# A convolution stack: the ninth tap's image in packed rows of 32 instead of a pitch of 34

## The chip, the core and the metric

The kernel runs on one core of a Trainium2 chip. The metric is the device time in microseconds of one execution; lower is better. In the profile PE is TensorE's matmul, PEld its weight load, DVE is VectorE, ACT is ScalarE, POOL is GpSimd and SP is SyncE.

## The reference

Four layers with residuals run on an image x of shape (4, 32, 32, 16). The first three are the same computation with their own weights:

```python
first = jnp.einsum('ijpq,bpqc->bijc', M2, inputs)
K = jnp.transpose(G, (2, 3, 4, 0, 1, 5)).reshape(kh, kw, c, h * w * f)
shifted = lax.conv_general_dilated(inputs, K, window_strides=(1, 1), padding='SAME', ...)
shifted = shifted.reshape(b, h, w, h, w, f)
diff = jax.nn.relu(inputs[:, :, :, None, None, :] - shifted)
second = jnp.einsum('ijpq,bpqijc->bijc', W2, diff)
return first - L * second
```

The inputs are group-normalised first. So there is, for each of the 1024 output places (i, j), a 3x3 convolution of the whole image with its own kernel G, a ReLU of its difference to the image, and a weighted sum over all 1024 places (p, q). The convolution has 9 taps x 16 channels, 144 rows of contraction, and 1024 x 16 output columns for each of the 4 images of the batch. The fourth layer filters with an impulse response obtained from Fourier transforms; it is a small part of the time.

## The kernel before

A layer runs over 128 blocks of 8 places and, within a block, over the 4 images of the batch: 512 steps a layer, 1536 in the three layers. One step (lines 533 to 558) fills a pair of PSUM banks, one bank for each half of the image (16 rows x 32 columns, 512 columns of output), and VectorE then does the minimum, the multiplication with the weights and the sum in one instruction, L550. Four such pairs of banks rotate.

The 144 rows of contraction don't fit 128 partitions, and the two halves of the image lie in the two halves of the partitions (rows 0 to 63 and 64 to 127, 4 taps x 16 channels each). So a step has three groups of matmuls, written at L542: `ga` with image tile 0 (taps 0, 1, 3, 4), `gb` with image tile 1 (taps 2, 5, 6, 7), both float32, and `gn` with image tile 2 for the ninth tap. The ninth tap alone would leave three quarters of its 64 rows unused; they hold its high and low pieces, so that gn can run in the reduced type float32r: slots of 16 rows with high, low, high, low pieces of the image meet high, high, low, low pieces of the weights (`prepare_g` cuts the weights, L464 and L468).

An image tile, `ims[a][k]`, belongs to a pair of images a = 0 or 1 and has the shape `[P, 4, 2, 4, 34]`: per partition 4 groups of rows l, 2 images b, 4 rows cc in a group, and a row of 34 floats. A matmul reads 32 of the 34: `rhs=im[rows, :, b % 2, :, :S]`, 4 x 4 rows of 32.

For layer 0 the host delivers the shifted images unnormalised in `raw`; `load_first` loads them on SP's queue, the ninth tap into a tile `nine`, and `first_images` normalises them. `last_tap` does the ninth on VectorE in three operations (L231, L233, L235), after which GpSimd clears the edges (L222). For layers 1 and 2 `make_image` does the work once for each pair a: `group_norm`, then `store_image`, then `load_image`. `store_image` normalises (L330), writes into `ys[a]` the image (`whole`, ACT), its high piece (DVE) and its low piece (DVE), each with a column of zeros on either side, copies the rows that neighbouring partitions need into `ye[a]` (POOL for one edge, ACT for the other), and stores both in DRAM as `img[a]`, `[10, C, 3, ROW]` with ROW = 2 x 4 x 34 = 272, on the queues of SP and ACT. `load_image` issues 24 loads in turn on the queues of SP, ACT and POOL; each brings one tap for one half from DRAM. The shift in x comes from the start of the read, `tap % 3`, the shift in y from the row of `img[a]`; 270 floats (RUN) for each l come as one run, the zeros between rows included.

The order of instructions is that of the code (a manual schedule). At a layer's end the last block is done for images 0 and 1 first and then for 2 and 3, and the first block of the next layer likewise, so the new image of pair 0 is made while TensorE works on pair 1 of the old layer, and the image of pair 1 while it works on pair 0 of the new one. `todo` and `step` thread these generators between the steps. `ys` and `ye` are zeroed once, in `impulse_response`.

Of the kernel before, what the change touches and what calls it, by code (L numbers as in the profile page):

```python
# [29 lines left out]
F32 = mybir.dt.float32  # L30
F32R = mybir.dt.float32r
AF = mybir.ActivationFunctionType
ALU = mybir.AluOpType
# [4 lines left out]
P = 128  # L38
B, C, S = 4, 16, 32
NBLK = 128  # L40
TAPS = [0, 1, 3, 4, 2, 5, 6, 7, 8]
ROW = 2 * 4 * 34
RUN = ROW - 2
GC = 8
NK = S // 2
NF = S * NK
# [9 lines left out]
def conv_stack_kernel(ctx, tc, x, raw, M, W, first_w, G, h0, coef, cst, dft, idp, idq, out):  # L56
    nc = tc.nc

    const = ctx.enter_context(tc.tile_pool(name="const", bufs=1))
# [3 lines left out]
    imp = ctx.enter_context(tc.tile_pool(name="image", bufs=1))  # L63
# [4 lines left out]
    dram = ctx.enter_context(tc.tile_pool(name="dram", bufs=1, space=DRAM))  # L68
# [19 lines left out]

    ys, ye, img = [], [], []
    for a in range(2):  # L90
        ys.append(const.tile([P, 3, 2, 4, 34], F32, name=f"y{a}"))
        ye.append(const.tile([P, 3, 2, 4, 34], F32, name=f"e{a}"))
        img.append(dram.tile([10, C, 3, ROW], F32, name=f"img{a}"))
    hd = dram.tile([8 + C * HLEN], F32, name="hd")
    fd = dram.tile([P, B, 2, 2, S], F32, name="fd")
    td = dram.tile([NK, 2, S, 2 * P], F32, name="td")
# [76 lines left out]
    ims, yc = {}, {}  # L173

    def image_tiles(a):


        ims[a] = [
            imp.tile([P, 4, 2, 4, 34], d, tag=f"im{a}{k}", name=f"im{a}{k}")
            for k, d in enumerate((F32, F32, F32R))  # L180
        ]

    def load_first(a, which, b=slice(0, 2)):

        if a not in ims:
            image_tiles(a)
            nine[a] = st.tile([P, 4, 2, 4, 34], F32, name=f"nine{a}")
        to = nine[a] if which == 2 else ims[a][which]
        nc.sync.dma_start(
            out=to[:, :, b].rearrange("p l b cc x -> p l (b cc x)"),  # L190
            in_=raw[:, a, which].rearrange("p (l b n) -> p l b n", l=4, b=2)[:, :, b].rearrange(
                "p l b n -> p l (b n)"
            ),
        )
# [131 lines left out]
    def normalise(a, xt, neg, rstd):  # L326
        yc[a] = work.tile([P, 2, NBLK], F32, tag=f"yc{a}", name=f"yc{a}")
        for b in range(2):
            at = slice(b, b + 1)
            nc.vector.tensor_scalar(yc[a][:, b], xt[:, b], neg[:, at], rstd[:, at], ALU.add, ALU.mult)  # L330

    def make_image(a, xt):

        xt = xt[:, 2 * a : 2 * a + 2]
        neg, rstd = yield from group_norm(xt)
        store_image(a, xt, neg, rstd)
        yield
        load_image(a)

    def store_image(a, xt, neg, rstd):  # L340
        split = lambda t: t.rearrange("p b (cc q) -> p b cc q", q=S)
        whole, hi, lo = (ys[a][:, k, :, :, 1:33] for k in range(3))
        normalise(a, xt, neg, rstd)
        y = yc[a]
        nc.vector.tensor_copy(hi.bitcast(F32R), split(y))
        nc.scalar.copy(whole, split(y))
        nc.vector.tensor_tensor(lo, split(y), hi, ALU.subtract)  # L347
        nc.gpsimd.tensor_copy(ye[a][96:, :, :, 1:, :], ys[a][96:, :, :, :3, :])  # L348
        nc.scalar.copy(ye[a][:32, :, :, :3, :], ys[a][:32, :, :, 1:, :])
        flat = lambda t: t.rearrange("p k b cc x -> p (k b cc x)")  # L350
        rows = img[a].rearrange("p c k x -> p c (k x)")
        nc.sync.dma_start(out=rows[1:9].rearrange("p c x -> (p c) x"), in_=flat(ys[a]))
        nc.scalar.dma_start(out=rows[0], in_=flat(ye[a][7 * C :]))
        nc.scalar.dma_start(out=rows[9], in_=flat(ye[a][:C]))

    def load_image(a):
        image_tiles(a)
        taps = [(n // 4, n % 4, 0, TAPS[n]) for n in range(8)]
        taps += [(2, n, 1 + n % 2, 8) for n in range(4)]
        jobs = [(half, *tap) for tap in taps for half in range(2)]  # L360

        jobs.sort(key=lambda job: job[4] // 3 == 2 * job[0])
        for n, (half, k, slot, which, tap) in enumerate(jobs):
            at, p = 64 * half + C * slot, 4 * half + tap // 3
            (nc.sync, nc.scalar, nc.gpsimd)[n % 3].dma_start(  # L365
                out=ims[a][k][at : at + C]
                .bitcast(F32)
                .rearrange("c l b cc x -> c l (b cc x)")[:, :, :RUN],
                in_=img[a][p : p + 4, :, which, tap % 3 : tap % 3 + RUN].rearrange(
                    "l c x -> c l x"  # L370
                ),
            )

    def load_m(mt, layer, pm):
# [3 lines left out]
    def first_term(layer, xt):  # L378

        ft = work.tile([P, 2, 8, S], F32, tag="ft", name="ft")  # L380
        with tc.tile_pool(name="mp", bufs=4) as mp:
# [10 lines left out]
            for pm in range(4, 8):  # L392
# [3 lines left out]
                yield  # L396
            for _ in range(GC - 4):
                yield
# [31 lines left out]
    def chunk(layer, ch):  # L430
        return layer + ch // (NBLK // GC), ch % (NBLK // GC)

    def load_g(layer, ch, parts=((slice(0, GC), "9ab", nc.sync, nc.sync, nc.sync),)):

        layer, ch = at = chunk(layer, ch)
        if layer == 3 or at in gr:
            return
        gr[at] = ga, gb, g9 = [
            pool.tile([P, GC, P], F32, tag=tag, name=tag) for pool, tag in ((gs, "ga"), (gs, "gb"), (gp, "g9"))
        ]  # L440
        flat = lambda t: t.rearrange("r n m -> r (n m)")
        operands = dict(zip("9ab", zip((g9, ga, gb), G[layer][ch])))
        for part, order, *queues in parts:
            for (t, src), queue in zip((operands[k] for k in order), queues):
                queue.dma_start(out=flat(t[:, part]), in_=src[:, part.start * P : part.stop * P])
                yield

    def prepare_g(layer, ch, part=slice(0, GC), engine=nc.gpsimd):


        at = chunk(layer, ch)
        if at[0] == 3 or (part.start == 0 and at in gt):
            return
        if part.start == 0:
            gt[at] = *gr[at][:2], gs.tile([P, GC, P], F32R, tag="gn", name="gn")
        ga, gb, gn = (t[:, part] for t in gt[at])
        g9 = gr[at][2][:, part]

        gv = ga.rearrange("r n (p f) -> r (n p) f", f=C)
        engine.tensor_tensor(  # L460
            gv, gv, mid.unsqueeze(1).to_broadcast([P, gv.shape[1], C]), ALU.subtract
        )
        yield
        nc.scalar.copy(gn, g9)  # L464
        yield
        for r in (32, 96):
            lo = gn[r : r + 32]
            nc.vector.tensor_tensor(lo, g9[r : r + 32], lo.bitcast(F32), ALU.subtract)  # L468
            yield
# [266 lines left out]
    nine = {}  # L736
    with tc.tile_pool(name="st", bufs=1) as st:
# [17 lines left out]
        for which in range(3):  # L755
            load_first(0, which, slice(0, 1))
        next(loads)
        for which in range(3):
            load_first(0, which, slice(1, 2))
# [4 lines left out]
        for which in range(3):  # L764
            load_first(1, which)
# [24 lines left out]
    def own(k, slot):  # L790

        y = lambda at: lambda cc: late["y3"][:, cc, at : at + 8]
        return [
            ("po" if tile == block else block, tile, y(31 - TQ * k - q + 8 * block), k, q)
            for tile, block, q in slot
        ]
# [13 lines left out]
    whole = [own(0, [(t, t, q) for t in range(4)]) for q in (2, 3)]  # L810
# [138 lines left out]
    for block in range(1, 4):  # L949
        for bank, tile in sorted(m for m in left if m[0] == block):  # L950
            row = xo[32 * block : 32 * block + 32].rearrange("n (r j) -> n r j", j=C)
            src = bank_of[block][32 * tile : 32 * tile + 32].rearrange("n (j r) -> n r j", j=C)
# [131 lines left out]
```

## Time and profile before

| | us |
|---|---|
| median of 3 runs | 3104.75 (3104.68 to 3104.94) |
| span of the profiled execution | 3103.0 |
| VectorE L550, mean of one (1536 of them) | 1.224 |
| its accumulator's read | 0.083 |
| ga, gb: TensorE records, mean | 0.590, 0.588 |
| gn: TensorE records, mean | 0.805 |
| weight loads of ga, gb, gn, mean | 0.187, 0.185, 0.186 |
| layers 1 and 2, `img` to `im` loads: 96 of 67.5 KB, from issue to landing | 5.4 median, 2.2 to 7.5 |
| store of `ys`: 4 of 408 KB, from issue to landing | 2.4 median |

The profile was taken in one execution, whose span lies 1.75 us below the median of the runs. A record of a matmul is longer than the time that it occupies the array, because successive matmuls overlap, and its end is modelled; the distance between starts tells what a pass takes. The two halves of a step run beside each other, some nanoseconds apart, so a pair of records is one pass. In a timeline each line has start, duration, engine, line, operation, operands and, in brackets, idle time before it with what ended it. TensorE's clock is granted in full throughout.

### The profile page before, as it was taken

To read this page: it belongs to the slowest core of one execution; us is meant where nothing else is said; L and a number is where in the kernel's file an instruction comes from. 1 tells how busy PE (TensorE), PEld (TensorE's weight loads), DVE (VectorE), ACT (ScalarE), POOL (GpSimd) and SP (SyncE) were. 2 spreads that over 40 slices of the span, in tenths; PEclk is the share of its full clock that TensorE was granted. 3 is DMA by queue.
4 is the path that set the end of the run, shared out by engine and by line. 5 is a ranking of instruction groups with operands and counts; after the bars stand their busy time and mean duration, and the time that the engine had idled before them with its cause. 6 is when DMAs were issued, how large, how long until landed. Compare 5 with 4: busy or idle time off the path is not lost.

```text
span 3103.0 us, 39162 instructions
## 1 busy us (share of the span) xinstructions
PE 3094.0 (100%) x16268; PEld 1618.2 (52%) x16268; DVE 2066.7 (67%) x3358; ACT 74.2 (2%) x93; POOL 239.6 (8%) x279
## 2 busy tenths in 40 slices
PE   9999999999999999999999999999999999999999
PEld 7854555555555554544545454555444545445454
DVE  7667666666667765666666666776666666666664
ACT  1000000000000000000000000000000000000000
POOL 1022220000000101000000000010100000000000
PEclk9999999999999999999999999999999999999999
DMA  7353443333332745333333333274644454445422
GB/s 231 102 146 89 108 115 95 89 89 95 102 89 62 158 129 129 89 89 95 102 89 89 95 102 89 62 152 128 144 100 97 100 113 104 97 95 119 95 44 42
DMA packets 71003, 322.46 MB, mean 104 GB/s; under 512 B 10409, under 2 KB 20393, under 8 KB 45481
## 3 DMA queue, kind: packets, MB, share of 16 engines
q1 hardware_dynamic: 60592, 302.24, 39.2%
q10 hardware_dynamic: 6152, 9.99, 1.8%
q0 software_dynamic: 4080, 7.72, 1.2%
q8 instruction: 127, 2.08, 0.3%
q14 instruction: 52, 0.42, 0.1%
HBM read 313.64 MB, written 6.28 MB: 103 GB/s over the span
## 4 chain that ended last, share of the span: by engine, by line
PE 100%; DMA 0%; DVE 0%; issue 0%; ACTq 0%; DVEq 0%; ACT 0%
PE pt L542 97%; PE pt L822 1%; PE pt L402 1%; PE pt L576 0%; DMA ga<-in_G_dram 0%; PE pt L649 0%; DVE junk L550 0%; PE pt L690 0%; PE pt L248 0%; DVE ga L460 0%; PE pt L121 0%; ACTq L81 0%; DVE xo L959 0%; DVE d L150 0%; DVE d L153 0%
## 5 line engine op out<-in xcount | busy, mean ns | idle before, releaser
L550 DVE SCALAR_TENSOR_TENSOR junk<-pt,w 128x1024 f32<-128x1024 f32 x1536 | 1880.6, 1224 | 989.0 <-PE pt L542 971.7
L542 PE MATMUL pt<-im,ga 64*128 64x512 f32 x6144 | 1607.4, 590 | 0.0
L542 PE MATMUL pt<-im,gb 64*128 64x512 f32 x6144 | 1600.6, 588 | 0.0
L542 PE MATMUL pt<-im,gn 64*128 64x512 f32 x3072 | 1276.0, 805 | 0.0
L542 PEld LDWEIGHTS pt<-im,gb 64*128 64x128 f32 x6144 | 636.7, 185 | 682.6 <-issue 672.4
L542 PEld LDWEIGHTS pt<-im,ga 64*128 64x128 f32 x6144 | 626.4, 187 | 409.2 <-DVE junk L550 278.3
L542 PEld LDWEIGHTS pt<-im,gn 64*128 64x128 f32 x3072 | 319.7, 186 | 340.3 <-issue 328.5
L460 POOL TENSOR_TENSOR ga<-ga,cs 128x1024 f32<-128x1024 f32 (+1 forms) x48 | 112.5, 2345 | 2025.8 <-DMA ga<-in_G_dram 2025.0
L550 DVE DVE_READ_ACCUMULATOR junk<-pt,w 128x1 f32 x1536 | 127.6, 83 | 0.0
L468 DVE TENSOR_TENSOR gn<-g,gn 32x1024 fp32r<-32x1024 f32 (+2 forms) x98 | 117.7, 1201 | 2.7 <-ACT gn L464 0.6
L464 ACT CAST gn<-g 128x1024 fp32r<-128x1024 f32 (+2 forms) x49 | 50.4, 1029 | 2256.5 <-PE pt L542 2088.2
L417 POOL DMA_DIRECT2D fd<-ft x48 | 25.3, 533 | 318.2 <-ACT ft L409 307.5
L822 PE MATMUL pt<-t,y 128*32 128x512 f32 (+3 forms) x352 | 23.9, 432 | 0.0
L705 POOL COPY hs<-v 32x512 f32<-32x512 f32 x16 | 17.1, 1072 | 47.2 <-ACT v L699 46.6
L946 DVE TENSOR_TENSOR xo<-xo,both 128x512 f32<-128x512 f32 x2 | 1.4, 692 | 26.7 <-DMA both<-sd 26.7
L822 PEld LDWEIGHTS pt<-t,y 128*32 128x32 f32 x352 | 10.9, 110 | 12.8 <-issue 10.9
L365 POOL DMA_DIRECT2D im<-img x32 | 16.1, 513 | 9.3 <-PE pt L542 6.6
L620 POOL TENSOR_TENSOR H<-H,d 128x256 f32<-128x256 f32 x8 | 6.8, 850 | 93.2 <-DVE d L625 92.9
L822 PE MATMUL pt<-t,yp 128*32 128x512 f32 (+3 forms) x192 | 13.6, 434 | 0.0
L348 POOL COPY e<-y 32x612 f32<-32x612 f32 x4 | 2.8, 692 | 129.4 <-DVE y L347 129.4
L402 PE MATMUL pt<-mt,yt 128*64 128x512 f32 x48 | 11.0, 599 | 0.0
L402 PE MATMUL pt<-w,yt 128*64 128x512 f32 x48 | 10.8, 592 | 0.0
(107 smaller groups left out, 192.5 us busy)
## 6 DMA issues: line engine op xcount, KB each, us to landing
w<-in_W_dram SPq DMA_DIRECT2D x188, 1024.0 KB, 7.5
g<-in_G_dram SPq DMA_DIRECT2D x47, 512.0 KB, 7.8
ga<-in_G_dram SPq DMA_DIRECT2D x47, 512.0 KB, 3.5
gb<-in_G_dram SPq DMA_DIRECT2D x47, 512.0 KB, 5.4
mt<-in_M_dram SPq DMA_DIRECT2D x12, 512.0 KB, 9.6
w<-in_M_dram SPq DMA_DIRECT2D x12, 512.0 KB, 4.1
t<-hd ACTq DMA_DIRECT2D x28, 160.0 KB, 7.8
t<-hd SPq DMA_DIRECT2D x28, 160.0 KB, 8.8
```

What stands on the lines that cost most here:

```text
L348: nc.gpsimd.tensor_copy(ye[a][96:, :, :, 1:, :], ys[a][96:, :, :, :3, :])
L365: (nc.sync, nc.scalar, nc.gpsimd)[n % 3].dma_start(out=ims[a][k][at : at + C] .bitcast(F32) .rearrange("c l b cc x -> c l (b cc x)")[:, :, ...
L402: nc.tensor.matmul(pf[64 * h : 64 * h + 64], lhsT=yt[:, k].rearrange("k b c -> k (b c)"), rhs=mt[:, bass.ts(h, 512)], start=(k == 0), stop ...
L417: nc.gpsimd.dma_start(out=fv[h, cc, b], in_=ft[at : at + C, cc])
L460: engine.tensor_tensor(gv, gv, mid.unsqueeze(1).to_broadcast([P, gv.shape[1], C]), ALU.subtract)
L464: nc.scalar.copy(gn, g9)
L468: nc.vector.tensor_tensor(lo, g9[r : r + 32], lo.bitcast(F32), ALU.subtract)
L542: nc.tensor.matmul(pt[:, half, :], lhsT=w[rows, blk % GC, :], rhs=im[rows, :, b % 2, :, :S], start=n == 0, stop=n == 2,)
L550: nc.vector.scalar_tensor_tensor(junk, pt.rearrange("p h m -> p (h m)"), 0.0, wt, ALU.min, ALU.mult, accum_out=acc[b // 2][:, b % 2, blk : ...
L620: mul = lambda o, u, w: nc.gpsimd.tensor_tensor(o, u, w, ALU.mult)
L705: nc.gpsimd.tensor_copy(hs[quarter[u], :, bass.ts(c, 8)], v[quarter[c], bass.ts(u, 8)].rearrange("q p m -> q m p"),)
L822: nc.tensor.matmul(rows.rearrange("n (j r) -> n j r", j=C)[:, :, 8 * cc :], lhsT=y(cc).rearrange("p q b -> p (q b)"), rhs=ts[k][q][:, :, : ...
```

## The change

The ninth tap's image is stored, loaded and read in rows of 32 without padding. Its shift in x, which for the ninth tap is always one column, is put in when the high and low pieces are written: columns 1 to 31 of the image go to columns 0 to 30, and column 31 stays zero. The tile of image 2 and the tile `nine` become `[P, 4, 2, 4, 32]`. `ys`, `ye` and `img` change from three equal parts of 272 floats to one part of 272 (the whole image, for the other taps) and two of 256 (NINE, the pieces). The edge rows are copied for the two kinds of part separately, so one copy on POOL becomes two, and one on ACT becomes two. `load_image` reads 256 floats in place of 270 for the ninth tap, from a fixed start. The matmuls' code is unchanged; its operand is now dense within each l. The host packs `raw` in the same manner.

```diff
+NINE = 2 * 4 * 32
...
-        ys.append(const.tile([P, 3, 2, 4, 34], F32, name=f"y{a}"))
-        ye.append(const.tile([P, 3, 2, 4, 34], F32, name=f"e{a}"))
-        img.append(dram.tile([10, C, 3, ROW], F32, name=f"img{a}"))
+        ys.append(const.tile([P, ROW + 2 * NINE], F32, name=f"y{a}"))
+        ye.append(const.tile([P, ROW + 2 * NINE], F32, name=f"e{a}"))
+        img.append(dram.tile([10, C, ROW + 2 * NINE], F32, name=f"img{a}"))
...
-            imp.tile([P, 4, 2, 4, 34], d, tag=f"im{a}{k}", name=f"im{a}{k}")
-            for k, d in enumerate((F32, F32, F32R))
+            imp.tile([P, 4, 2, 4, x], d, tag=f"im{a}{k}", name=f"im{a}{k}")
+            for k, (d, x) in enumerate(((F32, 34), (F32, 34), (F32R, S)))
...
-            nine[a] = st.tile([P, 4, 2, 4, 34], F32, name=f"nine{a}")
+            nine[a] = st.tile([P, 4, 2, 4, S], F32, name=f"nine{a}")
         to = nine[a] if which == 2 else ims[a][which]
+        src = raw[:, a, 4 * ROW * which :][:, : 4 * (NINE if which == 2 else ROW)]
...
+    def in_kinds(t):
+
+        whole = t[:, :ROW].rearrange("p (b cc x) -> p b cc x", b=2, cc=4)
+        pieces = t[:, ROW:].rearrange("p (k b cc x) -> p k b cc x", k=2, b=2, cc=4)
+        return whole, pieces[:, 0], pieces[:, 1]
+
+    def in_rows(t):
+
+        return (
+            t[:, :ROW].rearrange("p (b cc x) -> p b cc x", b=2, cc=4),
+            t[:, ROW:].rearrange("p (kb cc x) -> p kb cc x", kb=4, cc=4),
+        )
...
-        whole, hi, lo = (ys[a][:, k, :, :, 1:33] for k in range(3))
         normalise(a, xt, neg, rstd)
-        y = yc[a]
-        nc.vector.tensor_copy(hi.bitcast(F32R), split(y))
-        nc.scalar.copy(whole, split(y))
-        nc.vector.tensor_tensor(lo, split(y), hi, ALU.subtract)
-        nc.gpsimd.tensor_copy(ye[a][96:, :, :, 1:, :], ys[a][96:, :, :, :3, :])
-        nc.scalar.copy(ye[a][:32, :, :, :3, :], ys[a][:32, :, :, 1:, :])
...
+        y = yc[a].rearrange("p b (cc q) -> p b cc q", q=S)
+        whole, hi, lo = in_kinds(ys[a])
+        hi, lo = hi[..., : S - 1], lo[..., : S - 1]
+        nc.vector.tensor_copy(hi.bitcast(F32R), y[..., 1:])
+        nc.scalar.copy(whole[..., 1:33], y)
+        nc.vector.tensor_tensor(lo, y[..., 1:], hi, ALU.subtract)
+        for e, v in zip(in_rows(ye[a]), in_rows(ys[a])):
+            nc.gpsimd.tensor_copy(e[96:, :, 1:, :], v[96:, :, :3, :])
+            nc.scalar.copy(e[:32, :, :3, :], v[:32, :, 1:, :])
...
+            start, size = (ROW + NINE * (which - 1), NINE) if which else (tap % 3, RUN)
             (nc.sync, nc.scalar, nc.gpsimd)[n % 3].dma_start(
                 out=ims[a][k][at : at + C]
                 .bitcast(F32)
-                .rearrange("c l b cc x -> c l (b cc x)")[:, :, :RUN],
-                in_=img[a][p : p + 4, :, which, tap % 3 : tap % 3 + RUN].rearrange(
-                    "l c x -> c l x"
-                ),
+                .rearrange("c l b cc x -> c l (b cc x)")[:, :, :size],
+                in_=img[a][p : p + 4, :, start : start + size].rearrange("l c x -> c l x"),
             )
```

More of the change, by code (lines that the diff above doesn't have):

```diff
@@ L186, in load_first @@
             image_tiles(a)
-            nine[a] = st.tile([P, 4, 2, 4, 34], F32, name=f"nine{a}")
+            nine[a] = st.tile([P, 4, 2, 4, S], F32, name=f"nine{a}")
         to = nine[a] if which == 2 else ims[a][which]
+        src = raw[:, a, 4 * ROW * which :][:, : 4 * (NINE if which == 2 else ROW)]
         nc.sync.dma_start(
             out=to[:, :, b].rearrange("p l b cc x -> p l (b cc x)"),
-            in_=raw[:, a, which].rearrange("p (l b n) -> p l b n", l=4, b=2)[:, :, b].rearrange(
+            in_=src.rearrange("p (l b n) -> p l b n", l=4, b=2)[:, :, b].rearrange(
                 "p l b n -> p l (b n)"
@@ L338, in make_image @@
         load_image(a)
+    def in_kinds(t):
[7 more added lines that the diff above has]
+        )
     def store_image(a, xt, neg, rstd):
-        split = lambda t: t.rearrange("p b (cc q) -> p b cc q", q=S)
-        whole, hi, lo = (ys[a][:, k, :, :, 1:33] for k in range(3))
         normalise(a, xt, neg, rstd)
-        y = yc[a]
-        nc.vector.tensor_copy(hi.bitcast(F32R), split(y))
-        nc.scalar.copy(whole, split(y))
-        nc.vector.tensor_tensor(lo, split(y), hi, ALU.subtract)
-        nc.gpsimd.tensor_copy(ye[a][96:, :, :, 1:, :], ys[a][96:, :, :, :3, :])
[L349 to L354, printed above, removed]
+        y = yc[a].rearrange("p b (cc q) -> p b cc q", q=S)
[7 more added lines that the diff above has]
+            nc.scalar.copy(e[:32, :, :3, :], v[:32, :, 1:, :])
+        rows = img[a]
+        nc.sync.dma_start(out=rows[1:9].rearrange("p c x -> (p c) x"), in_=ys[a])
+        nc.scalar.dma_start(out=rows[0], in_=ye[a][7 * C :])
+        nc.scalar.dma_start(out=rows[9], in_=ye[a][:C])
     def load_image(a):
@@ L1033 @@
         raw[:, n % 4, :, :, n // 4, :, :, :, :S] = v.transpose(3, 6, 0, 4, 1, 2, 5)
+    raw = raw.reshape(P, 2, 3, -1, 34)
+    raw = [raw[:, :, 0], raw[:, :, 1], raw[:, :, 2, :, :S]]
+    raw = np.concatenate([v.reshape(P, 2, -1) for v in raw], 2)
     arrays = {
         "x": x.reshape(B, 4, 8, S, C).transpose(2, 4, 0, 1, 3).reshape(P, B, NBLK),
-        "raw": raw.reshape(P, 2, 3, -1),
+        "raw": raw,
     }
```

## The prediction

> **What bounds the kernel now.** I read the page first (busy time, chain, groups), then the chain of waits in order of time, then the timeline of one step in the middle of a layer, of one step at a layer's end, and of the store of an image.
>
> The page:
>
> ```profile
> PE 3094.0 (100%) x16268; PEld 1618.2 (52%) x16268; DVE 2066.7 (67%) x3358; ACT 74.2 (2%) x93; POOL 239.6 (8%) x279
> PEclk9999999999999999999999999999999999999999
> PE 100%; DMA 0%; DVE 0%; issue 0%; ACTq 0%; DVEq 0%; ACT 0%
> L550 DVE SCALAR_TENSOR_TENSOR junk<-pt,w 128x1024 f32<-128x1024 f32 x1536 | 1880.6, 1224 | 989.0 <-PE pt L542 971.7
> L542 PE MATMUL pt<-im,ga 64*128 64x512 f32 x6144 | 1607.4, 590 | 0.0
> L542 PE MATMUL pt<-im,gb 64*128 64x512 f32 x6144 | 1600.6, 588 | 0.0
> L542 PE MATMUL pt<-im,gn 64*128 64x512 f32 x3072 | 1276.0, 805 | 0.0
> ```
>
> The chain is TensorE from end to end, at the full clock, and nearly all of it is line 542. VectorE's L550 runs once per step, 1536 times, and waits for TensorE before it (972 us). A step has ga and gb, four records each (two passes for each half of the partitions), and gn, two records (one pass for each half). The ninth tap is gn's moving operand, and only that operand changes.
>
> The chain in order of time, one undisturbed stretch:
>
> ```profile
> 1201.40 813.02 PE pt L542 x4140
> ```
>
> 4140 records are 414 steps of ten, so a step takes 813.02 / 414 = 1.9638 us. One step in the timeline (start, duration, engine):
>
> ```profile
> 1503.78 1.03 PE L542 MATMUL pt<-im,ga 64*128 64x512 f32 x4
> ...
> 1504.64 1.03 PE L542 MATMUL pt<-im,gb 64*128 64x512 f32 x4
> ...
> 1505.07 0.20 PEld L542 LDWEIGHTS pt<-im,gn 64*128 64x128 f32 x2 [0.23 <-issue]
> 1505.10 0.81 PE L542 MATMUL pt<-im,gn 64*128 64x512 f32 x2
> ...
> 1505.50 0.44 PEld L542 LDWEIGHTS pt<-im,ga 64*128 64x128 f32 x4 [0.23 <-DVE junk L550]
> 1505.75 1.03 PE L542 MATMUL pt<-im,ga 64*128 64x512 f32 x4
> ```
>
> ga starts at 1503.78 and gb at 1504.64: 0.86 us for two passes, 0.43 each. gb's second pass starts at 1505.07 with the weight load for gn; the weight load for the next ga comes one more pass later, at 1505.50. A load starts when the pass before its own begins to stream, so gn streams from 1505.50, whatever the start of its record says, and the next ga streams from 1505.75. gn has the array for about 0.25 us. Averaging starts over 1512 undisturbed steps gives 433, 428, 429 and 673 ns for ga to second pass, to gb, to its second pass, and to the next ga. With 429 for gb's second pass, **gn takes 244 ns**.
>
> Is that the next weight load showing through? At a layer's end a small matmul of the same type stands between:
>
> ```profile
> 1001.09 0.20 PEld L121 LDWEIGHTS pt<-pieces,avg_r 64*128 64x128 f32 x2 [0.22 <-issue]
> ...
> 1001.34 0.19 PE L121 MATMUL pt<-pieces,avg_r 64*128 64x16 f32 x2
> 1001.34 0.32 PEld L542 LDWEIGHTS pt<-im,ga 64*128 64x128 f32 x4
> 1001.37 1.10 PE L542 MATMUL pt<-im,ga 64*128 64x512 f32 x3
> ```
>
> Four loads of 0.19 us fit in 0.32 us: the last begins at 1001.47, and the halves stand 0.02 apart, so ga's first pass streams about 0.11 us after its first load began. A load hides behind 0.11 us of streaming; it doesn't set 0.244. And here an fp32r matmul follows gn, and its start at 1001.34 is again 0.25 after its load: leaving fp32r for fp32 isn't the cost either.
>
> [...]
>
> **The change part by part.**
>
> 1. *gn's moving operand.* It goes from 16 rows of 32 at a pitch of 34 to 4 runs of 128 (the four l, 256 floats apart; rows within an l now touch). The record of L346, whose source is whole rows side by side, carries one run of 256, so I take it that these rows merge as well. What does a row cost? [...] Three candidates: a price per row end (12 of 16 go[...]); a price for rows off a 16-byte line (all become aligned[...]); a fixed price of a long fp32r pass (0). I take the price per row end[...]. Sum: 1536 x 21.1 = **32.4 us** off[...]. All of it lies on the chain. The next in line is late by nothing: VectorE needs 1.224 + 0.083 = 1.31 us a step against 1.943, the weight load 0.11 against 0.22.
>
> 2. *First images (layer 0).* The first of nine's loads are 256 KB for 272, and L231, L233 and L235 treat 512 instead of 544 elements: L231 and L233 take 0.56 us for 544 today, about 1 ns an element, so 0.03 us less each. Three of them stand before the first gn (its load waits 0.50 us for the clearing memset behind L235): 0.1 us off. The clearing memsets keep their size.
>
> 3. *Storing the image (4 times in the run: two halves, layers 1 and 2).* The hi cast and the subtraction cover 31 columns, 248 elements for 256: nothing. The edge copies become two on POOL and two on ACT:
>
> ```profile
> 1011.09 0.70 ACT L349 COPY e<-y 32x612 f32<-32x612 f32 x1 [0.43 <-DVE y L347]
> 1011.88 0.33 ACTq L353 DMA_DIRECT2D img<-e  x1
> ```
>
>    L346 takes 0.406 us for 256 elements and L349 0.704 for 612: 0.84 ns an element, 0.19 fixed. 204 + 384 elements in two copies: 0.88 us, so 0.17 more, before the two stores on ACT's queue and the loads behind them; POOL alike, about 0.15. The image's stores shrink from 408 to 392 KB, the eight loads of the ninth tap from 67.5 to 64 KB, with as many descriptors; SP, ACT and POOL issue eight loads each as before. So the image is complete about 0.2 us later. For the first half the loads are issued from 1013.5 to 1020.0, land by about 1027 (at most 7.5 us each), and the next layer reads them from 1033; for the second half they end at 1052.5, land by 1060, and are read after 16 steps from 1033, at 1064.6. Cover is 5.5 us and 4.6 us; price **0**. With the cover gone it would be at most 4 x 0.2 = 0.8 us.
>
> 4. *Clearing.* The four memsets of stores and edges on POOL have 784 columns for 816, off the chain: 0. TensorE's operands ga, gb and their images are untouched.
>
> Sum on the profiled execution: 3103.0 - 32.4 - 0.1 = 3070.5 us of span; the median of the runs lies 1.75 us above the span, so 3072.2.
>
> **Rivals.**
>
> *A, price per row end: 3072* (3066 to 3080, for 10 to 14 of 16 rows' price and a few us of scatter). [...] Against: no record here shows the same type without rows.
>
> *B, the whole excess goes: 3061.4.* [...]
>
> *C, fixed price: 3104.6.* If a 512-column fp32r pass takes 244 ns by itself[...], the step stays. [...]
>
> *D, slower: the packed image makes reads collide.* [...] The place is gn's pass, with the next ga's load beside it from 1505.50 on. It decides from a gn of over 244 ns: each 10 ns more cost 1536 x 0.01 = 15.4 us. At the outer end, the 429 ns of an fp32 pass, it would be 3104.75 + 1536 x 0.185 = 3389; my value is 10 ns, 3120. [...] Against: the weight loads last 185 to 187 ns beside every kind of pass, also beside the packed 256 columns of L576, so nothing here has ever been seen to collide.
>
> *E, the change doesn't reach TensorE:* if the operand kept three dimensions and the price hung on them, not on addresses; its time is C's, and I count it there.
>
> **How the numbers follow.** A 0.44, B 0.25, C with E 0.16, D 0.15. The forecast is A's, 3072. What this measurement can tell from no change is 0.2%, 6.2 us. Faster is A and B, 0.69; same is C, 0.16; slower is D, 0.15. The range reaches from B with 4 us below it, 3057, to C with a little above, 3107, and leaves out D; A's own is 3066 to 3080.
>
> **What would show it.** In the profile after, a step of L542 of 1.943 us (B: 1.936, C: 1.964), that is gb's second pass to the next ga 0.65 us instead of 0.67, with ga and gb passes still at 0.43; two edge copies per engine at the store; the loads of the images still landing before 1033 and 1064 less the shift. Wrong: a step that is unchanged, a gn over 0.25 us, or idle time on TensorE ahead of the first reads of a new image.

## The result and the profile after

The changed kernel takes 3079.49 us (median of 4 runs, 3079.29 to 3079.56) against 3104.72 us before (median of 4 runs): 25.2 us less, a ratio of 0.9918 with an interval of 0.9904 to 0.9932. The forecast was 3072, with a range of 3057 to 3107.

The page of the kernel after; matmuls are now at L556, VectorE's instruction at L564:

```profile
span 3077.5 us, 39162 instructions
PE 3068.5 (100%) x16268; PEld 1551.9 (50%) x16268; DVE 2066.5 (67%) x3358; ACT 74.8 (2%) x97; POOL 240.6 (8%) x283
PE 100%; DMA 0%; DVE 0%; issue 0%; ACTq 0%; DVEq 0%; ACT 0%
L564 DVE SCALAR_TENSOR_TENSOR junk<-pt,w 128x1024 f32<-128x1024 f32 x1536 | 1880.6, 1224 | 963.8 <-PE pt L556 940.6
L556 PE MATMUL pt<-im,ga 64*128 64x512 f32 x6144 | 1588.0, 588 | 0.0
L556 PE MATMUL pt<-im,gb 64*128 64x512 f32 x6144 | 1587.2, 588 | 0.0
L556 PE MATMUL pt<-im,gn 64*128 64x512 f32 x3072 | 1239.2, 790 | 0.0
```

TensorE still sets everything, at a granted clock of 1.000 as before, and the counts of its instructions are the same. VectorE has the same work and waits less for TensorE (940.6 us at L564, 971.7 at L550 before). The chain of waits in order of time, the same stretch of layer 1 as before:

```profile
1191.50 806.12 PE pt L556 x4140
```

414 steps of 1.9471 us, where there were 414 of 1.9638: 16.7 ns a step, and 1536 x 16.7 ns = 25.6 us. The spans differ by 25.5. So, within a few tenths of a microsecond, the whole result lies inside the step. One step in the timeline:

```profile
1503.86 1.02 PE L556 MATMUL pt<-im,gb 64*128 64x512 f32 x4
1504.29 0.19 PEld L556 LDWEIGHTS pt<-im,gn 64*128 64x128 f32 x2 [0.24 <-issue]
1504.31 0.80 PE L556 MATMUL pt<-im,gn 64*128 64x512 f32 x2
...
1504.72 0.42 PEld L556 LDWEIGHTS pt<-im,ga 64*128 64x128 f32 x4 [0.24 <-DVE junk L564]
1504.95 0.59 PE L556 MATMUL pt<-im,ga 64*128 64x512 f32 x2
```

gb's second pass starts at 1504.29, with the load for gn; the load for the next ga starts at 1504.72, with gn's pass; and that ga starts at 1504.95: gn has the array for 0.23 us instead of 0.25. Averages of starts over 1511 undisturbed steps: 429, 429, 429 and 660 ns, against 433, 428, 429 and 673 before. So gn went from 244 to 231 ns, and ga's first pass behind it from 433 to 429; the two are best taken together, as 1963.5 - 1946.9 = 16.6 ns a step.

The store of the first new image on ACT:

```profile
1001.92 0.41 ACT L361 COPY y<-yc 128x256 f32<-128x256 f32 x1 [2.88 <-DVE yc L332]
1002.36 0.85 ACT L365 COPY e<-y 32x204 f32<-32x204 f32 x2
1003.37 0.33 ACTq L368 DMA_DIRECT2D img<-e  x1
```

The two edge copies take 0.85 us for 0.70, but the first of them needs only the whole image, so it no longer waits 0.43 us for VectorE's low piece. The store is issued 1.45 us after the start of L361, before 1.63 us after L346. TensorE goes through the three layers without a gap, as before (no idle time before the matmuls of L556, and 97.2% of the chain in both profiles).

### The profile page after: what moved, and what is told of

It is laid out like the page before. It is cut to its first block, busy times and chain, and to the rows that moved or that the text cites. A ratio compares the mean times of both kernels' runs of the same rounds, so it can differ in the third digit from the quotient of the medians.

```text
span 3077.5 us, 39162 instructions
## 1 busy us (share of the span) xinstructions
PE 3068.5 (100%) x16268; PEld 1551.9 (50%) x16268; DVE 2066.5 (67%) x3358; ACT 74.8 (2%) x97; POOL 240.6 (8%) x283
## 4 chain that ended last, share of the span: by engine, by line
PE 100%; DMA 0%; DVE 0%; issue 0%; ACTq 0%; DVEq 0%; ACT 0%
PE pt L556 97%; PE pt L836 1%; PE pt L416 1%; PE pt L590 0%; DMA ga<-in_G_dram 0%; PE pt L663 0%; DVE junk L564 0%; PE pt L704 0%; PE pt L250 0%; DVE ga L474 0%; DVE xo L973 0%; ACTq L82 0%; PE pt L122 0%; DVE d L151 0%; DVE d L154 0%
## 5 line engine op out<-in xcount | busy, mean ns | idle before, releaser
L564 DVE SCALAR_TENSOR_TENSOR junk<-pt,w 128x1024 f32<-128x1024 f32 x1536 | 1880.6, 1224 | 963.8 <-PE pt L556 940.6
L556 PE MATMUL pt<-im,ga 64*128 64x512 f32 x6144 | 1588.0, 588 | 0.0
L556 PE MATMUL pt<-im,gb 64*128 64x512 f32 x6144 | 1587.2, 588 | 0.0
L556 PE MATMUL pt<-im,gn 64*128 64x512 f32 x3072 | 1239.2, 790 | 0.0
L556 PEld LDWEIGHTS pt<-im,gb 64*128 64x128 f32 x6144 | 613.5, 186 | 705.1 <-issue 695.1
L556 PEld LDWEIGHTS pt<-im,ga 64*128 64x128 f32 x6144 | 596.1, 186 | 414.8 <-DVE junk L564 290.5
L556 PEld LDWEIGHTS pt<-im,gn 64*128 64x128 f32 x3072 | 306.9, 186 | 353.0 <-issue 338.9
L564 DVE DVE_READ_ACCUMULATOR junk<-pt,w 128x1 f32 x1536 | 127.3, 83 | 0.0
L431 POOL DMA_DIRECT2D fd<-ft x48 | 25.2, 533 | 315.0 <-ACT ft L423 304.6
```

Source lines behind the costliest of these rows:

```text
L431: nc.gpsimd.dma_start(out=fv[h, cc, b], in_=ft[at : at + C, cc])
L556: nc.tensor.matmul(pt[:, half, :], lhsT=w[rows, blk % GC, :], rhs=im[rows, :, b % 2, :, :S], start=n == 0, stop=n == 2,)
L564: nc.vector.scalar_tensor_tensor(junk, pt.rearrange("p h m -> p (h m)"), 0.0, wt, ALU.min, ALU.mult, accum_out=acc[b // 2][:, b % 2, blk : ...
```

## The experiments

What in the packed rows shortens the pass? Below, a line is 4 floats, 16 bytes, counted from the start of a tile, a unit for telling the layouts apart, and a run of floats is a stretch of them side by side, without a hole. Theory E is the prediction's: a price for each end of such a run. Rival L is the second of its three candidates: a price for rows that start off a line. Theories H and N, in some expectations, are sizes given to L's price along the way. In the traces gn's operand is recorded as 32 x 4 x 4 floats before, and as 128 x 4 in the packed kernel: its rows do merge. All times are compared with the packed kernel's 3079.5 us, and steps are read from the chain of waits, layer 1, as above.

### Rows aligned but not touching: pitch 36

```diff
-NINE = 2 * 4 * 32
+NINE = 2 * 4 * 36
...
-            for k, (d, x) in enumerate(((F32, 34), (F32, 34), (F32R, S)))
+            for k, (d, x) in enumerate(((F32, 34), (F32, 34), (F32R, NINE // 8)))
```

The tile `nine`, the stores and loads of the pieces and the host's array widen with it; the matmul reads 32 of 36.

> Ninth tap's image at a pitch of 36 floats, so every row of 32 starts on a 16-byte line but no row touches the next (16 runs of 32). Theory E, a price per run end: as slow as a pitch of 34, a step of 1.963 us, about 3104 us. Rival L, a price for rows that start off a 16-byte line: as fast as packed rows, a step of 1.947 us, about 3079 us.

3084.55 us (2 runs, ratio to before 0.9935, 0.9915 to 0.9955).

```profile
1193.54 807.51 PE pt L556 x4140
```

1.9505 us a step: 3.4 ns above packed, 13.3 below before. With all 16 row ends still there, four fifths of the gain are there too. Theory E's price falls from the prediction's 21.1 / 12 = 1.76 to at most 3.4 / 12 = 0.28 ns for each end; the rest comes with alignment. Rival L isn't exact either, for it allowed nothing for the ends.

### One run of 512

```diff
+        t = imp.tile([P, 2, 4, 4, S], F32R, tag=f"im{a}2", name=f"im{a}2")
+        ims[a].append(t.rearrange("p b l cc x -> p l b cc x"))
...
+            queue = (nc.sync, nc.scalar, nc.gpsimd)[n % 3]
+            for b in range(2 if which else 0):
+                queue.dma_start(
+                    out=ims[a][k][at : at + C, :, b].bitcast(F32).rearrange("c l cc x -> c l (cc x)"),
+                    in_=img[a][p : p + 4, :, start + 128 * b : start + 128 * b + 128].rearrange(
+                        "l c x -> c l x"
+                    ),
+                )
...
```

> The ninth tap's tile has the image index ahead of the row groups, so the moving operand of a step is one run of 512 floats instead of 4 of 128. Theory E: three run ends less at 1.39 ns (16.6 ns over the 12 that went), a step of 1.9427 us, about 3073 us. Rival L, all rows are aligned already: no change to the packed kernel, 3079 us. The load of a piece becomes two of half the size, off the chain in both.

3079.28 us (3079.16 to 3079.37, 4 runs) against 3079.29 to 3079.56 for the packed kernel.

```profile
1191.61 806.12 PE pt L568 x4139
```

The stretch lasts the same 806.12 us as packed. Going from 4 runs to 1 is worth nothing, which is Rival L's number; so the 3.4 ns of the pitch of 36 aren't a price per run end either, at least not one that holds for the last three. What they are isn't settled: the operand of the pitch of 36 has not only more runs, it also takes a dimension more to describe (32 x 4 x 4, against 128 x 4 packed and 512 here), and the two weren't tried apart.

### Rows off their lines on purpose

The tile gets 4 more floats per group, and the image begins 2 or 1 floats into it. All rows are then off a line; loads and stores keep their sizes, and the groups stand 4 floats further apart. With a pitch of 36:

```diff
+        t = imp.tile([P, 4, NINE + 4], F32R, tag=f"im{a}2", name=f"im{a}2")
+        t = t[:, :, 2 : NINE + 2]
+        ims[a].append(t.rearrange("p l (b cc x) -> p l b cc x", b=2, cc=4))
```

> Pitch of 36 floats, but the tile's rows begin 2 floats into a 16-byte line: all 16 rows of a step are off a line (8 of 16 at a pitch of 34). Theory H, a row that starts half a line in costs about 1.66 ns (at 34: 13.3 ns over 8 rows, above the 3.35 ns of the pitch of 36): 26.6 ns a step more than at a pitch of 36, a step of 1.977 us, about 3125 us, slower than before. Theory E, run ends alone count: as at a pitch of 36, 3084.5 us.

3122.93 us (3122.80 to 3123.10, 3 runs; ratio to before 1.0059, 1.0036 to 1.0082): slower than the kernel before, though each row has the same 32 floats.

```profile
1208.65 817.87 PE pt L559 x4140
```

1.9755 us: 25.0 ns above the pitch of 36, 1.56 ns for each of 16 rows. The same with `t[:, :, 1 : NINE + 1]`:

> Pitch of 36 floats, rows begin 1 float into a line: 16 rows with a first line of 3 floats and a last one of 1. If an extra line costs its whole time (33 or 35 would then have been slower than they were): 26.7 ns more than at 36, about 3125 us. If a half line (8 bytes) is what costs: half of that, 13.3 ns more, about 3105 us. Theory E: 3084.5 us.

3122.47 us (3122.45 to 3122.62, 3 runs).

```profile
1208.37 817.82 PE pt L559 x4140
```

The same to 0.1 ns a step. A first line with three floats used and a last one with one cost what two lines with two each cost: in both a row touches 9 lines instead of 8, and how many floats of the extra line are used made no difference here.

The packed rows, 2 floats into a line, give 4 runs off a line instead of 16:

> Packed rows, 4 runs of 128, but each run begins 2 floats into a 16-byte line; the DRAM side and all loads are as in the packed kernel. Theory H: 4 runs x 1.66 = 6.7 ns a step more than packed, a step of 1.9535 us, about 3090 us. Theory E: unchanged, 3079.5 us.

3086.81 us (3086.75 to 3086.84, 3 runs).

```profile
1194.43 808.22 PE pt L559 x4138
```

1.9522 us: 5.1 ns more than packed for 4 extra lines, 1.3 each. Theory E had no change here; it is refuted a second time. The 4 floats more between the groups weren't tried without the offset; the one run of 512, with its groups 128 floats apart instead of 256, shows no effect of their distance.

### Pitches of 33 and 35

> Ninth tap's image at a pitch of 33 floats: 16 runs of 32, 12 of them off a 16-byte line (8 of 16 at a pitch of 34), half of them off an 8-byte boundary too. Theory E: the step of a pitch of 34, 1.963 us, about 3104 us. Rival L: slower than the kernel before, 12/8 of the gain of 16.6 ns lost, a step of 1.972 us or more, about 3117 us or more.

3092.12 us (3092.08 to 3092.25, 3 runs): faster than the pitch of 34, where both theories had it at least as slow.

```profile
1196.62 809.55 PE pt L556 x3932
```

(This stretch, too, is 414 steps; where a count of records is lower, some are missing from the trace.) 12 of 16 rows are off a line instead of 8, and yet the step is 1.9554 us (809.55 / 414), 8.3 ns above packed. Neither the number of rows nor the number of rows off a line sets the price. What differs is that neighbouring rows with one float between them share a line: 33 lines are touched in each group of four rows, 34 at a pitch of 34. That count of lines was then tried at 35:

> Pitch of 35 floats. Rows start 0, 35, 70 and 105 floats into each group, and no two rows meet in a line of 4 floats: 35 lines are read per group, against 32 packed, 33 at a pitch of 33 (where neighbouring rows share a line) and 34 at a pitch of 34. Theory N, a line costs 4 columns (1.667 ns) however few of its floats are used, and a run end 0.28 ns (from the pitch of 36, 3.35 ns over 12): 12 extra lines and 12 run ends, 20.0 + 3.35 ns more than packed, a step of 1.970 us, about 3115 us, slower than before. Rival L, a price for each row that starts off a line, as many here as at 33: the time of 33, about 3092 us.

3104.89 us (10 runs; ratio to before 1.0001, 0.9991 to 1.0011), 1.9639 us a step (813.05 / 414).

```profile
1201.36 813.05 PE pt L556 x4139
```

Neither number came: a third of what 12 extra lines should have cost is missing. Put together, the lines that a step touches in each partition, the runs of floats, and ns above packed:

| rows of the ninth tap | lines | runs of floats | ns a step |
|---|---|---|---|
| packed | 128 | 4 | 0 |
| one run of 512 | 128 | 1 | 0.0 |
| pitch 36 | 128 | 16 | 3.4 |
| packed, 2 floats off | 132 | 4 | 5.1 |
| pitch 33 | 132 | 16 | 8.3 |
| pitch 34 (before) | 136 | 16 | 16.7 |
| pitch 35 | 140 | 16 | 16.7 |
| pitch 36, 1 or 2 floats off | 144 | 16 | 28.3, 28.4 |

The lines order the table, but for 34 and 35, which tie. Among the kernels with 16 runs of floats, above the pitch of 36, an extra line costs 1.2 (33), 1.7 (34), 1.1 (35) and 1.6 ns (36 off); four columns last 1.66 at the 0.416 ns of a column that the run with 384 columns, below, gives. So in these layouts extra lines went with 1.1 to 1.7 ns each; why the price of one varies, and 35 above all, stays unexplained.

### What is left of the pass

Four fp32 passes, 429.2 ns each by the starts in the profile after, leave 1946.9 - 4 x 429.2 = 230 ns for gn. The run with 384 columns, below, gives 0.416 ns for each column between 384 and 512. If that holds for all 512, they take 213 ns, and about 17 of the 230 don't go with the columns: an estimate from these two lengths alone. Are the 17 paid for changing the type, once a step? gn twice in a row:

```diff
-                    for n, (w, im) in enumerate(zip(gt[layer, blk // GC], ims[b // 2])):
+                    taps = list(zip(gt[layer, blk // GC], ims[b // 2]))
+                    for n, (w, im) in enumerate(taps + taps[2:]):
...
-                                stop=n == 2,
+                                stop=n == 3,
```

> Packed kernel with gn issued twice in a row in every step (the ninth tap counts twice): what a pass costs behind a pass of its own type. [...]the step grows by 230 ns to 2.177 us, about 3433 us. [...]

3437.3 us (1 run). In the timeline gn's second load is at 1600.43, the load for ga at 1600.66, ga at 1600.89: two passes of 0.23 each.

```profile
1600.03 1.03 PE L557 MATMUL pt<-im,gn 64*128 64x512 f32 x4
...
1600.43 0.19 PEld L557 LDWEIGHTS pt<-im,gn 64*128 64x128 f32 x2 [0.24 <-issue]
1600.66 0.42 PEld L557 LDWEIGHTS pt<-im,ga 64*128 64x128 f32 x4
1600.89 0.59 PE L557 MATMUL pt<-im,ga 64*128 64x512 f32 x2
```

```profile
1330.53 902.72 PE pt L557 x4968
```

The step grew by 902.72 / 414 - 1.9471 = 0.233 us, not by 0.213. Each pass pays, behind a float32 pass as behind one of its own type.

The next three have gn between ga and gb. The first changes nothing else; it asks whether the price lies in the start of the next group behind gn, and it is the reference of the other two:

```diff
+                    taps = list(zip(gt[layer, blk // GC], ims[b // 2]))
+                    for n, (w, im) in enumerate(taps[k] for k in (0, 2, 1)):
```

> Packed kernel with the order ga, gn, gb in each step. gn is no longer the pass ahead of the next group's first matmul. [...]unchanged, a step of 1.947 us, 3079 us. [...] It is also the kernel to compare the next two with.

3080.18 us (1 run).

```profile
1192.40 806.12 PE pt L557 x4140
```

A step of 806.12 / 414 = 1.9471 us: unchanged, so the start of the next group has no part in it. Then with 384 columns:

```diff
-                                pt[:, half, :],
+                                pt[:, half, : 384 if n == 1 else 512],
...
-                                rhs=im[rows, :, b % 2, :, :S],
+                                rhs=im[rows, : 3 if n == 1 else 4, b % 2, :, :S],
```

> Order ga, gn, gb; gn covers only the first 384 of 512 columns of each half (the ninth tap is left out for the last group of rows). Against the same order with 512 columns: [...]128 x 0.4167 = 53.3 ns a step less, 82 us less, about 2998 us. [...]

2997.9 us (1 run).

```profile
2137.17 780.27 PE pt L557 x4120
```

412 steps of 1.8939 (this stretch is from layer 2): 53.2 ns less for 128 columns, 0.416 ns each. Had all of the pass gone with the columns, a quarter of it, 57.5 ns, would have gone; the difference, 4.3 ns, is a quarter of the estimated fixed part of 17. The weight load beside the pass doesn't set it either: gn now has the array for 230 - 53 = 177 ns, less than the 186 ns of a load. Last, gn for one half alone (`range(1 if n == 1 else 2)` for the halves):

> Order ga, gn, gb; gn only for the first half of the partitions (the ninth tap is left out for the other half of the image). [...]unchanged, 3079 us.

3079.56 us (1 run).

```profile
2196.20 805.69 PE pt L557 x3724
```

Within 1.0 ns unchanged, again in layer 2: 805.69 / 414 = 1.9461 us. So the 17 ns don't come from two gn passes side by side. The other half wasn't idle, though: by the records gn has its half from about 1601.54 (its load starts at 1601.11, with a float32 pass of 0.43) to about 1601.76 (the gb behind it ends at 1602.35, after 0.59), and in the other half a pass of gb starts in between, at 1601.64 (the first of the two records in the last line).

```profile
1601.13 0.79 PE L557 MATMUL pt<-im,gn 64*128 64x512 f32 x1
1601.64 0.71 PE L557 MATMUL pt<-im,gb 64*128 64x512 f32 x2
```

A gn with nothing at all beside it wasn't tried. So each pass of this type in this kernel has a part that didn't go with the columns, estimated at 17 ns; its origin wasn't found.

## Why the prediction was right, and where not

The bound, the place and the sign were right: gn's pass, read as 244 ns from starts alone, is what the change shortened, and no other wait took its place. The mechanism that gave the size was not, and that the time still came within 8 us of the forecast is in part luck.

The step that failed is in part 1, "I take the price per row end". Its term was 21.1 ns a step, 32.4 us; the step gained 16.7 ns, 25.6 us. The 21.1, like the excess that B speaks of, were an estimate of the author's: what gn takes without any price for its rows was in no trace. It was wrong in two places. First in kind: 16 aligned rows keep their ends and cost 3.4 ns together, while the extra lines of rows off a line make 13.3 ns of the 16.7 (pitch 34 against 36). A price for rows off a line was the prediction's second candidate. Second in size: a gn of 244 - 21.1 = 223 ns was expected, with 4 of 16 prices still to be paid, but with all rows aligned, in 4 runs or in 1, it takes 230, and about 17 of these are the fixed part, rival C's mechanism. What gn had to lose was not one thing with one price. (Nor was all of it in gn: of the 16.7 ns, about 4 are in ga's first pass, 433 ns before and 429 after.) A of the rivals came nearest in time by two errors of opposite sign: its price of a row, 1.76 ns, was too high, for the 16 rows lost 16.7 ns, 1.04 each; and it let the prices of 4 of 16 rows stay, where the one run of 512 found nothing left of them. B let too much of gn go (a step of 1.936 us), C nothing (1.964); it became 1.947.

Rival D, collision, didn't happen: weight loads last 186 ns (185 to 187 before). With an offset of 2 floats the packed image lost 5.1 ns of its gain, but was still faster than the rows of 34. Rival E is excluded by the step itself and by the merged rows in the operand's record.

Part 2, 0.1 us at the first gn: the first gn starts at 13.07 us against 13.18, of which about 0.05 was there before the images' work. That is too small to be told apart: the load of the first weights, which stands ahead of it on the chain, alone takes 4.14 us here, 4.18 before, and from 4.13 to 4.40 in the experiments where the chain shows it. Part 3, priced at nothing because of cover: the two copies on ACT take 0.15 us more (0.17 said) and the pair on POOL 0.88 against 0.69, TensorE doesn't wait, and the earlier start, which the prediction overlooked, gives it back. Part 4, the clearing, doesn't show.

## What to carry to other kernels

In a float32r pass like gn, try the moving operand with every row starting at a multiple of 16 bytes: packed it gained 16.7 ns a step here, and a padded pitch of a whole number of lines (36 floats) 13.3. With 16 separate rows an offset of one float cost more (25 ns) than packing had gained. Before sharing an excess out over one cause, vary the length: 384 columns against 512 showed a part that didn't go with the columns. The float32 passes ga and gb take 429 ns at a pitch of 34; a packed image for them wasn't tried.

## What the runs showed of the hardware

The moving operand's layout in memory set the time of a float32r pass of the same 512 columns. The three layouts whose rows all start at a multiple of 4 floats gave steps of 1.9471 us (packed and one run of 512) and 1.9505 us (pitch 36); all others, from 1.9522 us (packed, 2 floats off) to 1.9755 us (pitch 36, 2 floats off). A line more went with 1.1 to 1.7 ns. Between the two offsets at a pitch of 36 it made no difference how many floats of the partly used lines were read: 1.9755 us a step with two and two, 1.9754 with three and one, 1.56 ns more for each row than with none off. And with the best layout tried such a pass takes 230 ns for 512 columns, at 0.416 ns for each column between 384 and 512; a part of about 17 ns, an estimate from these two lengths, doesn't go with the columns. A float32 pass of the same kernel takes 429 ns for its 512 columns; what part of it is fixed wasn't tried.
